# Gated cross-attention with a mixture of experts: score products in six single PSUM buffers, exponentials and maxima head by head, the two kinds of products interleaved

## The chip, the cores and the metric

The kernel runs on one core of a Trainium2 chip. A core has engines with instruction streams of their own: TensorE (PE in the profile; PEld are its weight loads), VectorE (DVE), ScalarE (ACT), GpSimd (POOL) and SyncE (SP, which here issues most DMAs). They wait for each other through semaphores. PE writes its products to PSUM, eight banks of 512 fp32 values in each of 128 partitions, and DVE and ACT read them from there. The metric is the device time of one execution in microseconds (us), as the median over runs.

## The reference, cut to what matters

```python
def reference(x, ctx_2048, g_xattn, g_ffn, ...):      # x, ctx: (8, 256, 512)
    x = x + tanh(g_xattn) * xattn(layernorm(x), ctx_2048, ctx_2048, ...)
    x = x + tanh(g_ffn) * moe(layernorm(x), ...)

def xattn(query, key, value, ...):                     # 16 heads of 16, sequence 512
    q, k, v = proj(Wq, query), proj(Wk, key), proj(Wv, value)
    q, k = rotary(q), rotary(k)
    scores = einsum('bdhn,bdhm->bhnm', q, k) / sqrt(16)
    prob = softmax(scores, axis=-1)
    x = einsum('bhnm,bdhm->bdhn', prob, v)
    return proj(Wm, x)

def moe(x, ...):                                       # 2048 tokens, 8 experts, top 2
    ...
    h = silu(x @ w0[e]) * (x @ w1[e]);  out += cw[e] * (h @ wo[e])
```

All is fp32. The softmax takes 8 x 16 heads with a 512 x 512 score matrix each.

## The kernel before

The kernel has two long stages: attention with routing (to about 605 us in the profile) and the experts (the rest). The change is in the first.

**Units and steps.** The 128 pairs of batch and head are cut into 32 units of four heads. The four heads of a unit lie on partitions 0, 32, 64 and 96 ("slots"), so that their products, whose contraction is over 32 partitions, sit in different rows of PE's array. A unit takes four steps, one for each block of 128 queries (or, in the second pass, of 128 keys). There are 128 steps. A batch is 16 steps.

**Two passes over the scores.** `scores(u, i, jp)` multiplies queries by keys for two heads (L803) and takes the maximum over the keys on DVE (L810, `tensor_reduce`, negated, into `nm`). `lower(u)` turns the maxima of a unit (L824) and sends them by four small DMAs (L827) into a spare row of the queries `qa`. `exponentials(u, mc, jp)` computes the scores again, transposed and with the maximum already subtracted by that row (L838), and ACT takes the exponential (L845) into `e`. `attend(u, mc)` multiplies `e` by the values and a column of ones (L855). The second pass runs `LAG` = 5 steps behind the first.

**Order by hand.** The loop at L1311 writes the order out, inside `manual_schedule`. Each step `t` has three places. Place 0 and place 1 end with one group of four score products: `exponentials` for two heads of the older unit, then `scores` for the two other heads of the newer unit, so that the four use all four slots:

```python
exponentials(t2 // NCH, t2 % NCH, place)
...
scores(t // NCH, t % NCH, 1 - place)
```

Ahead of each place stands other work, filed by `do(step, place, fn, ...)` and issued by `run`: its products first, then the rest. `attend` stands at place 1. At place 2 there is mostly one pair of projection, value or merge products (`turn` L610, `values` L780, `merge` L900) or transposes (`turn_half` L818) into the single bank `m`, evicted by ACT. On DVE the other work is: `attend`'s transposition of its result (L867), at place 1 once a unit; `normalise` (L878, L881) and `lower` (L824), at place 2 once a unit; `turn_back` (L891), at place 1 every second unit; `query_stats` and `token_stats` (L176, L177), one at place 1 and one at place 2, each once a batch; `own_both` (two instructions, L658) at place 2 twice a batch; and the router's small operations (L990 to L1087).

**PSUM.** The pool `ps_s` has three buffers of two banks each. A call of `scores` or `exponentials` takes one of them, fills both halves with two products, and has them read by one instruction of 1024 elements: the maximum or the exponential. Two further banks are `m` and `av`. Thus the buffer of a `scores` call is the one that the `exponentials` call of the group just before it had, and the buffer of an `exponentials` call is the one that the `scores` call two groups before had. `pair()` and `bank()` take from the same pool for the start, for the early expert rows and after the last step.

Of the kernel before, what the change touches and what calls it, by code (L numbers as in the profile page):

```python
# [8 lines left out]
FP = mybir.dt.float32  # L9
AF = mybir.ActivationFunctionType  # L10
ALU = mybir.AluOpType
AX = mybir.AxisListType
PSUM = bass.MemoryType.PSUM

P = 128
B, C, N = 8, 256, 512
H, HD = 16, 16
HG = P // HD
NG = H // HG
SLOT = 32  # L20
NS = P // SLOT
CC = C // P
NCH = N // P
UNITS = 2 * NG
E, M = 8, 1024
# [11 lines left out]
MOST, LEAST = max(CAPS), min(CAPS)  # L37
WHOLE = -(-MOST // SLOT) * SLOT
CT = MOST // P
# [12 lines left out]
def gated_cross_attention_moe(  # L52
# [19 lines left out]
    nc = tc.nc  # L72
# [19 lines left out]

    gw = const.tile([P, DC, SLOT], FP, tag="gw", name="gw")
    nc.gpsimd.memset(gw, 0.0)
    total = const.tile([P, E], FP, tag="total", name="total")
    nc.gpsimd.memset(total, 0.0)
    for i in range(NS):
# [5 lines left out]
            1.0,  # L103
            base=-i * SLOT,
            channel_multiplier=1,
# [37 lines left out]
    for par in range(2):  # L143
        nc.gpsimd.affine_select(
            spare[:, par, :],
            spare[:, par, :],
            [[-SLOT, NS]],
            ALU.not_equal,
# [82 lines left out]
    def tiles_of(n_rows):  # L231
        return [(j, min(P, n_rows - j * P)) for j in range(-(-n_rows // P))]
# [3 lines left out]
    class Rows:  # L236


        def __init__(self, pool, at, n_rows, most=0, once=None):
            self.n_rows, self.turned = n_rows, 0  # L240
            self.tiles = tiles_of(n_rows)
            self.n_blocks = -(-n_rows // SLOT)
            n_blocks = -(-max(most, n_rows) // SLOT)
# [191 lines left out]
    with ExitStack() as fill:  # L435
# [7 lines left out]
        r1 = prep.enter_context(tc.tile_pool(name="prep_1", bufs=1, side="right"))  # L443
        r2 = prep.enter_context(tc.tile_pool(name="prep_2", bufs=2, side="right"))
        r3 = prep.enter_context(tc.tile_pool(name="prep_3", bufs=3, side="right"))
        ps_s = fill.enter_context(tc.tile_pool(name="ps_s", bufs=3, space=PSUM, side="right"))
        ps_1 = ps_att.enter_context(tc.tile_pool(name="ps_1", bufs=1, space=PSUM))

        nobody = r1.tile([P, ROW], FP, tag="nobody", name="nobody")
# [9 lines left out]
        nm = wp.tile([P, NCH, 2, NS], FP, tag="nm", name="nm")  # L459
# [35 lines left out]
        others = p4.tile([P, NS, N], FP, tag="e", name="others")  # L495
# [31 lines left out]

        whole = slice(0, N)
        halves = slice(0, N // 2), slice(N // 2, N)
        banks = []  # L530
        spared = [False]
        where = ["m"]

        def bank():


            if not banks:
                if spared[0]:
                    banks.append(ps_s.tile([P, 2, N], FP, tag="s", name="s")[:, 0, :])
                else:  # L540
                    banks.append(ps_1.tile([P, N], FP, tag=where[0], name=where[0]))
            return banks[0]
# [20 lines left out]
        def constant_bias():  # L563

            ps = bank()
            for c in range(CC):
                for g in range(NG):
                    nc.tensor.matmul(
# [3 lines left out]
                        start=(g == 0),  # L572
                        stop=(g == NG - 1),
                    )
# [7 lines left out]
        xns, straight, turned, qs, ks, keys = {}, {}, {}, {}, {}, {}  # L582
        qas, es, avs_, outs, ats, pays = {}, {}, {}, {}, {}, {}
# [207 lines left out]
        def slot(j):  # L791
            return slice(j * SLOT, (j + 1) * SLOT)

        def spare_of(u):
            return HD * (1 - u % 2)

        def scores(u, i, jp):

            q, k = qs[u], ks[u]
            ps = ps_s.tile([P, 2, N], FP, tag="s", name="s")  # L800
            for j in range(2):
                sl = slot(2 * jp + j)
                nc.tensor.matmul(  # L803
                    ps[:, j, :],
                    lhsT=q[sl, i * P : (i + 1) * P],
                    rhs=k[sl, :],
                    start=True,
                    stop=True,
                )
            nc.vector.tensor_reduce(  # L810
                nm[:, i, u % 2, 2 * jp : 2 * jp + 2], ps, AX.X, ALU.max, negate=True
            )

        def turn_half(src, h, at=None):

# [13 lines left out]
                    in_=t[u % 2 * NS + j :: 2 * NS, :],  # L829
                )  # L830

        def exponentials(u, mc, jp):
            if (u, mc) not in es:
                es[u, mc] = p4.tile([P, NS, N], FP, tag="e", name="e")
            ps = ps_s.tile([P, 2, N], FP, tag="s", name="s")
            for j in range(2):
                sl = slot(2 * jp + j)
                nc.tensor.matmul(  # L838
                    ps[:, j, :],
                    lhsT=ks[u][sl, mc * P : (mc + 1) * P],  # L840
                    rhs=qas[u][sl, :],
                    start=True,
                    stop=True,
                )
            nc.scalar.activation(  # L845
                es[u, mc][:, 2 * jp : 2 * jp + 2, :], ps, AF.Exp, scale=float(HD**-0.5)
            )

        def attend(u, mc):
            b, g, par = u // UNITS, u // 2 % 2, u % 2  # L850
# [44 lines left out]
        def merge(b, c, cols):  # L895

            x_t = xres[b * CC + c]
            ps = bank()[:, : cols.stop - cols.start]
            for g in range(NG):
                nc.tensor.matmul(  # L900
# [3 lines left out]
                    start=(g == 0),  # L904
                    stop=(g == NG - 1),
                )
# [211 lines left out]
        LAG = NCH + 1  # L1118
        group_turns = ("k", 0), ("q", 0), ("k", 1), ("q", 1)
        for b in range(B):  # L1120
            t = b * per_batch


            if b:
                do(t - 16, 1, loads, b)
                i, i2 = (-14, -12) if b == 1 else (-15, -15)
# [14 lines left out]
            at = (-8, -7, -6, 1) if b == 1 else (-10, -9, -8, 1)  # L1141
            if b == 0:
                at = (3, 3, 4, 5)
            for mc, i in enumerate(at):
                do(t + i, 2 if b or mc == 1 else 1, values, b, mc, halves[0])
            for w in range(UNITS):
                u = UNITS * b + w
                s = t + w * NCH
# [9 lines left out]
            s = t + per_batch + LAG + 3  # L1158
            if b + 2 == B:
# [9 lines left out]
                at = "8.1 8.1 8.2 8.2 9.1 10.1 10.1 10.2 10.2 11.1"  # L1169
            else:  # L1170
# [8 lines left out]
                at = "15.1 15.2 16.1 16.2 17.1 17.2 18.1 18.2 19.1 19.2"  # L1179
# [29 lines left out]
        for i in range(3):  # L1209
            for c in range(NCH):  # L1210
                at = i * NCH + c
                do(2 * per_batch + at // 2 * NCH + at % 2, 0, part_of_weights, i, c)
        n_steps = B * per_batch
# [4 lines left out]
        t = AHEAD * per_batch + per_batch + LAG + 3  # L1218
# [75 lines left out]
            return t.unsqueeze(2 if t is limit else 1).to_broadcast(all_tiles)  # L1294

        def pair():
            ps = ps_s.tile([P, 2, N], FP, tag="s", name="s")
            return ps[:, 0, :], ps[:, 1, :]

        def early_work():  # L1300
            wg, wu, wout = firsts[0]
            r = early["rows"]
            yield from r.hidden(wg, wu, early["pool"], early["sg"], 1, pair, later)
            yield from r.project(wout, r.weights(0), lambda: pair()[0])
# [5 lines left out]
        with tc.manual_schedule():  # L1310
            for t in range(min(k[0] for k in beside), max(k[0] for k in beside) + 1):  # L1311
                for place in range(3):
                    spared[0] = t >= n_steps
                    where[0] = "av" if t < LAG and place == 2 else "m"
                    run(beside.pop((t, place), ()))
                    if place == 2:
                        continue
                    t2 = t - LAG
                    if 0 <= t2 < n_steps:
                        if t < n_steps:  # L1320
                            exponentials(t2 // NCH, t2 % NCH, place)
                        elif place == 0:
                            for jp in range(2):
                                exponentials(t2 // NCH, t2 % NCH, jp)
                    if LAG <= t < n_steps:
                        scores(t // NCH, t % NCH, 1 - place)
                    elif 0 <= t < LAG and place == 0:
                        for jp in range(2):
                            scores(t // NCH, t % NCH, jp)

            spared[0] = False
            b = B - 1
            work = early_work()
            normalise(UNITS * B - 1)
            turn_back(b, NG - 1)
            go(4)
            alone(merge, b, 0, whole)
            go(1)
            alone(merge, b, 1, whole)
            for c in range(CC):  # L1340
                token_stats(b, c)
            go(3)

            fn, args = held.pop(0)
            fn(*args)
            for c in range(CC):
                token_norm(b, c)
            go(6)
            full(token_turn, b, 0)
            go(1)  # L1350
            full(token_turn, b, 1)
            go(1)
            alone(consider, b)
            go(1)
            alone(choose, b)
            for fn, *args in router:
                if fn is count:
                    go(5)
                run([(fn, (b, *args))])
            holding[0] = False  # L1360
            flush()
            att.close()
            ps_att.close()

            w_odd = ctx.enter_context(tc.tile_pool(name="w_odd", bufs=1, reuse_waits="tile"))
            arrange()

            nc.vector.tensor_tensor(over, *map(by_tile, (limit, step)), ALU.add)
            nc.vector.tensor_tensor(
                lefts, taken.unsqueeze(2).to_broadcast(all_tiles), over, ALU.subtract  # L1370
            )
            nc.vector.tensor_scalar(there, lefts, 0.0, None, ALU.is_gt)
            nc.vector.tensor_reduce(n_over, there, AX.XY, ALU.add)
            nc.vector.tensor_copy(n_over_i, n_over)

            go(17)
# [359 lines left out]
```

## Time and profile before

| | |
|---|---|
| median of 3 runs | 1248.45 us (1246.9 to 1248.92) |
| the profiled execution's own time | 1244.89 us |
| its span, first to last instruction | 1243.2 us |
| granted PE clock | 0.996 of full |
| busy, share of the span | PE 98%, DVE 70%, PEld 60%, POOL 44%, ACT 35% |
| attention, 90 to 520 us: busy of 430 us | PE 429.8, DVE 325.7, ACT 254.5, POOL 183.6 |

PE is called busy from a product's start to its modelled end, so a product that waits while another runs beside it does not show as idle time. Shares over the whole span mix the two stages: DVE and ACT work most in the attention.

### The profile page before, as it was taken

To read this page: it belongs to the slowest core of one execution; us is meant where nothing else is said; L and a number is where in the kernel's file an instruction comes from. 1 tells how busy PE (TensorE), PEld (TensorE's weight loads), DVE (VectorE), ACT (ScalarE), POOL (GpSimd) and SP (SyncE) were. 2 spreads that over 40 slices of the span, in tenths; PEclk is the share of its full clock that TensorE was granted. 3 is DMA by queue.
4 is the path that set the end of the run, shared out by engine and by line. 5 is a ranking of instruction groups with operands and counts; after the bars stand their busy time and mean duration, and the time that the engine had idled before them with its cause. 6 is when DMAs were issued, how large, how long until landed. Compare 5 with 4: busy or idle time off the path is not lost. (4 is left out here: it accounts for less than half of the span.)

```text
span 1243.2 us, 18455 instructions
## 1 busy us (share of the span) xinstructions
PE 1221.7 (98%) x6768; PEld 747.8 (60%) x6768; DVE 869.2 (70%) x1638; ACT 431.2 (35%) x652; POOL 545.2 (44%) x654
## 2 busy tenths in 40 slices
PE   8999999999999999999999999999999999999996
PEld 5433343343433334333455778888888888888885
DVE  7676778777787777877432486686876868777673
ACT  3555655655565565655510110110101102021110
POOL 5413444515354360712122491754917548192631
PEclk9999999999999999999999999999999999999998
DMA  7440133312011110102155711621526126060100
GB/s 225 171 130 18 35 120 120 117 41 83 19 61 60 53 61 18 62 10 70 52 205 143 249 46 44 245 48 68 206 52 254 35 97 209 24 246 12 55 1 33
DMA packets 70651, 117.98 MB, mean 95 GB/s; under 512 B 14480, under 2 KB 33168, under 8 KB 70560
## 3 DMA queue, kind: packets, MB, share of 16 engines
q1 hardware_dynamic: 62528, 91.47, 22.7%
q0 software_dynamic: 8032, 25.32, 5.5%
q8 instruction: 54, 0.88, 0.3%
q14 instruction: 37, 0.30, 0.1%
HBM read 78.19 MB, written 31.00 MB: 88 GB/s over the span
## 5 line engine op out<-in xcount | busy, mean ns | idle before, releaser
L810 DVE TENSOR_REDUCE nm<-s 128x2 f32<-128x1024 f32 x256 | 311.1, 1220 | 131.1 <-PE s L803 130.9
L845 ACT ACTIVATE e<-s 128x1024 f32<-128x1024 f32 x256 | 261.5, 1023 | 183.7 <-PE s L838 101.1
L838 PE MATMUL s<-qa,k 32*128 32x512 f32 x1024 | 288.0, 639 | 1.4 <-DMA qa<-turned 1.3
L803 PE MATMUL s<-k,q 32*128 32x512 f32 x1024 | 283.6, 639 | 1.5 <-DVE q L658 1.0
L1516 PE MATMUL h<-hT,w 128*128 128x256 f32 (+4 forms) x672 | 168.0, 386 | 0.0
L1527 DVE TENSOR_TENSOR c<-u,h 128x256 f32<-128x256 f32 (+4 forms) x280 | 117.0, 423 | 71.8 <-PE h L1516 64.7
L838 PEld LDWEIGHTS s<-qa,k 32*128 32x128 f32 x1024 | 78.3, 183 | 146.7 <-issue 119.4
L415 POOL DMA_INDIRECT out_x<-y,tail x37 | 40.6, 1097 | 275.9 <-DVE y L1607 170.5
L1516 PEld LDWEIGHTS h<-hT,w 128*128 128x128 f32 x672 | 127.2, 190 | 23.3 <-DVE c L1527 1.8
L1532 ACT COPY u<-h 128x256 f32<-128x256 f32 (+4 forms) x70 | 26.3, 375 | 329.5 <-PE h L1516 279.3
L855 PE MATMUL av<-e,vones 128*32 128x512 f32 x1024 | 137.3, 605 | 0.2 <-ACT e L845 0.2
L1527 DVE TENSOR_TENSOR u<-u,h 128x256 f32<-128x256 f32 (+4 forms) x210 | 87.4, 424 | 60.3 <-PE h L1516 56.8
L1516 PE MATMUL h<-sum_h,sum_w 128*128 128x256 f32 (+4 forms) x448 | 108.6, 385 | 0.0
L916 POOL TENSOR_TENSOR x<-x,mrg 128x512 f32<-128x512 f32 x14 | 17.9, 1277 | 195.2 <-ACT mrg L912 194.2
L1516 PEld LDWEIGHTS h<-sum_h,sum_w 128*128 128x128 f32 x448 | 85.1, 190 | 14.3
L1576 ACT ACTIVATE c<-c 128x256 f32<-128x256 f32 (+4 forms) x112 | 46.1, 423 | 128.2 <-DVE c L1527 128.1
L1579 DVE TENSOR_TENSOR act<-c,c 128x256 f32<-128x256 f32 (+4 forms) x112 | 84.4, 754 | 3.8
L803 PEld LDWEIGHTS s<-k,q 32*128 32x128 f32 x1024 | 75.9, 183 | 9.0 <-ACT e L845 4.2
L855 PEld LDWEIGHTS av<-e,vones 128*32 128x32 f32 x1024 | 20.3, 108 | 98.2 <-issue 77.4
L1516 PE MATMUL h<-wo,act 128*128 128x256 f32 x336 | 77.5, 380 | 0.0
L1516 PEld LDWEIGHTS h<-wo,act 128*128 128x128 f32 x336 | 63.5, 190 | 9.5 <-issue 1.0
L1516 PE MATMUL h<-hT,sum_w 128*128 128x256 f32 (+4 forms) x224 | 59.1, 386 | 0.8 <-DVE c L1527 0.8
(227 smaller groups left out, 1697.7 us busy)
## 6 DMA issues: line engine op xcount, KB each, us to landing
w<-in_w SPq DMA_DIRECT2D x14, 2048.0 KB, 10.5
wo<-in_wo SPq DMA_DIRECT2D x7, 2048.0 KB, 15.9
rows<-nobody SPq DMA_DIRECT2D x8, 1042.0 KB, 5.7
swapped<-straight SPq DMA_DIRECT2D x60, 128.0 KB, 2.0
ctx<-in_kv SPq DMA_DIRECT2D x8, 512.0 KB, 5.7
x<-in_x SPq DMA_DIRECT2D x16, 256.0 KB, 3.0
out_x<-x SPq DMA_DIRECT2D x16, 256.0 KB, 2.0
w<-in_w SPq DMA_DIRECT2D x8, 512.0 KB, 3.9
```

Source lines behind the costliest of these rows:

```text
L415: scatter = nc.gpsimd.indirect_dma_start(out=out_rows, out_offset=bass.IndirectOffsetOnAxis(ap=self.ids[j], axis=0), in_=self.ys[j][: self ...
L803: nc.tensor.matmul(ps[:, j, :], lhsT=q[sl, i * P : (i + 1) * P], rhs=k[sl, :], start=True, stop=True,)
L810: nc.vector.tensor_reduce(nm[:, i, u % 2, 2 * jp : 2 * jp + 2], ps, AX.X, ALU.max, negate=True)
L838: nc.tensor.matmul(ps[:, j, :], lhsT=ks[u][sl, mc * P : (mc + 1) * P], rhs=qas[u][sl, :], start=True, stop=True,)
L845: nc.scalar.activation(es[u, mc][:, 2 * jp : 2 * jp + 2, :], ps, AF.Exp, scale=float(HD**-0.5))
L855: nc.tensor.matmul(avs_[u][slot(j), :], lhsT=vones[b % 2][:, mc, g * HG + 2 * j + par, :], rhs=e[:, j, :], start=(mc == 0), stop=(mc == NC ...
L916: (nc.vector if b == B - 1 else nc.gpsimd).tensor_tensor(x_t, x_t, t, ALU.add)
L1516: nc.tensor.matmul(ps, lhsT=left[:, c], rhs=right[:, c], start=(c == 0), stop=(c == k - 1))
L1527: nc.vector.tensor_tensor(z, x, y, ALU.add)
L1532: nc.scalar.copy(u1, p1)
L1576: nc.scalar.activation(c, c, AF.Silu)
L1579: nc.vector.tensor_tensor(r.act[:, NS * i + q, j * n : (j + 1) * n], sg[i, j], c, ALU.mult)
```

## The change

The pool has six buffers (`RING`) of one bank each. `take(n)` takes n of them. `both` replaces a call of `exponentials` and one of `scores` in every step in which both passes run: it takes four buffers and issues the products in turn, one of the second pass (`again`), one of the first (`score`), then again one of each. Each buffer is read by an instruction of its own, of 512 elements: `exponential` on ACT and `largest_of` on DVE, head by head. Where only one pass runs, `scores` and `exponentials` do the same with two buffers. `pair()` gives two of the six buffers, and `bank()`, where it used half of a double buffer, takes two and uses one. Nothing else is touched, and the other work keeps its steps and places.

```diff
+RING = 6
...
-        ps_s = fill.enter_context(tc.tile_pool(name="ps_s", bufs=3, space=PSUM, side="right"))
+        ps_s = fill.enter_context(tc.tile_pool(name="ps_s", bufs=RING, space=PSUM, side="right"))
...
+        def take(n):
+            return [ps_s.tile([P, N], FP, tag="s", name="s") for _ in range(n)]
...
+        def score(u, i, j, at):
+            nc.tensor.matmul(at, lhsT=qs[u][slot(j), i * P : (i + 1) * P],
+                             rhs=ks[u][slot(j), :], start=True, stop=True)
+        def largest_of(u, i, j, at):
+            nc.vector.tensor_reduce(
+                nm[:, i, u % 2, j : j + 1], at, AX.X, ALU.max, negate=True
+            )
...
-            nc.vector.tensor_reduce(
-                nm[:, i, u % 2, 2 * jp : 2 * jp + 2], ps, AX.X, ALU.max, negate=True
-            )
...
+        def exponential(u, mc, j, at):
+            nc.scalar.activation(
+                es[u, mc][:, j, :], at, AF.Exp, scale=float(HD**-0.5)
+            )
...
-            nc.scalar.activation(
-                es[u, mc][:, 2 * jp : 2 * jp + 2, :], ps, AF.Exp, scale=float(HD**-0.5)
-            )
...
+        def both(u, mc, u2, i, jp):
+            at = take(NS)
+            js = 2 * jp, 2 * jp + 1
+            others = 2 - 2 * jp, 3 - 2 * jp
+            for k in range(2):
+                again(u, mc, js[k], at[2 * k])
+                score(u2, i, others[k], at[2 * k + 1])
+            for k in range(2):
+                exponential(u, mc, js[k], at[2 * k])
+                largest_of(u2, i, others[k], at[2 * k + 1])
...
+                    if LAG <= t < n_steps:
+                        both(t2 // NCH, t2 % NCH, t // NCH, t % NCH, place)
+                        continue
```

More of the change, by code (lines that the diff above doesn't have):

```diff
@@ L538, in bank @@
                 if spared[0]:
-                    banks.append(ps_s.tile([P, 2, N], FP, tag="s", name="s")[:, 0, :])
+                    banks.append(take(2)[0])
                 else:
@@ L795, in spare_of @@
             return HD * (1 - u % 2)
+        def score(u, i, j, at):
+            nc.tensor.matmul(
+                at,
+                lhsT=qs[u][slot(j), i * P : (i + 1) * P],
+                rhs=ks[u][slot(j), :],
+                start=True,
+                stop=True,
+            )
[3 more added lines that the diff above has]
+            )
         def scores(u, i, jp):
-            q, k = qs[u], ks[u]
-            ps = ps_s.tile([P, 2, N], FP, tag="s", name="s")
+            at = take(2)
             for j in range(2):
[L802 to L808, printed above, removed]
-                )
-            nc.vector.tensor_reduce(
-                nm[:, i, u % 2, 2 * jp : 2 * jp + 2], ps, AX.X, ALU.max, negate=True
-            )
+                score(u, i, 2 * jp + j, at[j])
+            for j in range(2):
+                largest_of(u, i, 2 * jp + j, at[j])
         def turn_half(src, h, at=None):
@@ L830, in lower, with again, exponentials @@
                 )
-        def exponentials(u, mc, jp):
+        def again(u, mc, j, at):
             if (u, mc) not in es:
                 es[u, mc] = p4.tile([P, NS, N], FP, tag="e", name="e")
-            ps = ps_s.tile([P, 2, N], FP, tag="s", name="s")
-            for j in range(2):
[L837 to L845, printed above, removed]
-                es[u, mc][:, 2 * jp : 2 * jp + 2, :], ps, AF.Exp, scale=float(HD**-0.5)
-            )
+            nc.tensor.matmul(
+                at,
+                lhsT=ks[u][slot(j), mc * P : (mc + 1) * P],
+                rhs=qas[u][slot(j), :],
+                start=True,
+                stop=True,
+            )
+        def exponential(u, mc, j, at):
+            nc.scalar.activation(
+                es[u, mc][:, j, :], at, AF.Exp, scale=float(HD**-0.5)
+            )
+        def exponentials(u, mc, jp):
+            at = take(2)
+            for j in range(2):
+                again(u, mc, 2 * jp + j, at[j])
+            for j in range(2):
+                exponential(u, mc, 2 * jp + j, at[j])
+        def both(u, mc, u2, i, jp):
[8 more added lines that the diff above has]
+                largest_of(u2, i, others[k], at[2 * k + 1])
         def attend(u, mc):
@@ L1296, in pair @@
         def pair():
-            ps = ps_s.tile([P, 2, N], FP, tag="s", name="s")
-            return ps[:, 0, :], ps[:, 1, :]
+            return take(2)
         def early_work():
@@ L1318, in gated_cross_attention_moe @@
                     t2 = t - LAG
+                    if LAG <= t < n_steps:
+                        both(t2 // NCH, t2 % NCH, t // NCH, t % NCH, place)
+                        continue
                     if 0 <= t2 < n_steps:
-                        if t < n_steps:
-                            exponentials(t2 // NCH, t2 % NCH, place)
-                        elif place == 0:
+                        if place == 0:
                             for jp in range(2):
                                 exponentials(t2 // NCH, t2 % NCH, jp)
-                    if LAG <= t < n_steps:
-                        scores(t // NCH, t % NCH, 1 - place)
-                    elif 0 <= t < LAG and place == 0:
+                    if 0 <= t < LAG and place == 0:
                         for jp in range(2):
```

## The prediction

> **What bounds the kernel now.** I read the page first: PE is busy 98% of the span, and the score groups are among its dearest.
>
> ```profile
> PE 1221.7 (98%) x6768; PEld 747.8 (60%) x6768; DVE 869.2 (70%) x1638; ACT 431.2 (35%) x652; POOL 545.2 (44%) x654
> ...
> L810 DVE TENSOR_REDUCE nm<-s 128x2 f32<-128x1024 f32 x256 | 311.1, 1220 | 131.1 <-PE s L803 130.9
> L845 ACT ACTIVATE e<-s 128x1024 f32<-128x1024 f32 x256 | 261.5, 1023 | 183.7 <-PE s L838 101.1
> L838 PE MATMUL s<-qa,k 32*128 32x512 f32 x1024 | 288.0, 639 | 1.4 <-DMA qa<-turned 1.3
> ```
>
> DVE and ACT each idle before the scores, waiting for PE. PE's own waits hide in its busy time, so the timeline comes next (start, duration). One step:
>
> ```profile
> 300.37 0.70 PE L838 MATMUL s<-qa,k 32*128 32x512 f32 x2
> 300.38 0.70 PE L803 MATMUL s<-k,q 32*128 32x512 f32 x2
> ...
> 301.44 1.06 PE L855 MATMUL av<-e,vones 128*32 128x512 f32 x8
> 301.63 1.02 ACT L845 ACTIVATE e<-s 128x1024 f32<-128x1024 f32 x1 [0.68 <-PE s L803]
> 301.63 1.23 DVE L810 TENSOR_REDUCE nm<-s 128x2 f32<-128x1024 f32 x1 [0.98 <-PE s L803]
> ...
> 302.43 0.70 PE L838 MATMUL s<-qa,k 32*128 32x512 f32 x2
> ...
> 302.70 0.70 PE L803 MATMUL s<-k,q 32*128 32x512 f32 x2
> ```
>
> At place 0 (300.37) both kinds of products start within 0.01 us, and the next block starts 1.07 later. At place 1 (302.43) the scores start 0.27 late, because their buffer is free only when ACT's exponential ends, at 301.63 + 1.02 = 302.65. The row shows 0.05 from that end to PE's start, and the whole group is late by the 0.27.
>
> I took the time from each group's first product to the next block, less 1.07, over PE's whole timeline from 30 to 585 us. The 123 groups at place 1 lose 26.6 us, 96 of them 0.2 to 0.3 each. The 122 at place 0 lose 10.2 us, 105 of them nothing. Between 90 and 520 us, six regular batches, it is 22.0 and 0.6; the ends have 4.3 (30 to 90) and 9.8 (520 to 585). So 37 us is all that the change can take away. The rest of a step is products.
>
> **The change, part by part.**
>
> *First buffers free sooner.* A group now takes four of six buffers. Its first two products need what the group two back released; the last two need the first exponential and the first maximum of the group just before. Both sides of that are new: PE waited for DVE two groups back, now one back.
>
> *Exponential of 512.* Not in the trace. A copy of 256 from PSUM takes 0.37 and the exponential of 1024 takes 1.02, so 512 takes between those; on the line through both, 0.59. It ends 1.26 (301.63 − 300.37) + 0.59 + 0.05 = 1.90 after its group's start. The next group needs it 2.06 later (302.43 − 300.37): the place 1 wait goes, with 0.16 to spare. ACT gets 128 x 2 x (1.18 − 1.02) = 41 us more busy time, but 254 of 430 us is its load in the regular stretch, so that is covered. Were the cover gone, it would be 0.16 a group.
>
> *Maximum of 512.* Bounds: the 16-element reduction of the router takes 0.17, that of 1024 1.22; the line gives 0.69 at 512. Other DVE rows of 512 are 0.67 (L176), 0.71 (L867). I take 0.69. The first maximum is done at 1.26 + 0.69 + 0.05 = 2.00: 0.06 to spare at place 1, if DVE is free when the product ends.
>
> *What two cost DVE.* Instructions overlap at their ends: below, a maximum starting at 359.20 and lasting 1.19 is followed at 360.31, not 360.39. From all such pairs in the trace, 1024 occupy DVE 1.14, so 512 occupy 1.14 − 512/0.96 ns = 0.61, two of them 1.21. A step without waits has period 4.43 − 0.27 ≈ 4.15, of which four maxima take 2.43. That leaves DVE holes of 0.85 (its place 1 maxima to the next place 0 maxima) and 0.85 for the other work, which comes in bursts:
>
> ```profile
> 357.79 0.71 DVE L867 STREAM_TRANSPOSE avs<-av 128x512 f32<-128x512 f32 x1
> 358.42 0.65 DVE L176 BATCH_NORM_STATS2 st<-x 128x6 f32<-128x512 f32 x1
> 359.10 0.18 DVE L177 BATCH_NORM_AGGREGATE mv<-st 128x2 f32<-128x6 f32 x1
> 359.20 1.19 DVE L810 TENSOR_REDUCE nm<-s 128x2 f32<-128x1024 f32 x1
> ...
> 360.31 0.68 DVE L176 BATCH_NORM_STATS2 st<-x 128x6 f32<-128x512 f32 x1
> ...
> 364.59 2.55 DVE L658 TENSOR_SCALAR q<-a,own_col 128x512 f32<-128x512 f32 x2
> ...
> 367.06 2.34 DVE L810 TENSOR_REDUCE nm<-s 128x2 f32<-128x1024 f32 x2
> ```
>
> Before, such a burst delayed a buffer needed two groups later and cost nothing: these steps keep their period (the own queries at 364.59 make DVE do two maxima in a row at 367.06, and PE does not wait). Now the fourth product of the next group waits behind it, with everything behind that product on PE. Worked per batch, with a hole of 0.85:
> - own queries (L658), the pair that runs while POOL rotates: 2.55 less the hole is 1.7 late, less the 0.06 and what the preceding hole absorbs: 1.3. The batch's other pair takes 0.48 + 0.48, and fits.
> - transposition and first statistics at place 1: 0.63 + 0.78 occupy 1.41; 0.56 late, 0.4 on PE. Then the second statistics and `normalise` at place 2, 1.4 again: 0.57 on PE. Together 1.0.
> - the same with `token_stats`, one hole freer: 0.7.
> - `lower` comes 3.75 before the next unit's first second-pass product, where it had 3.7 to 4.3; its DMAs issue 0.28 and 0.86, in one unit of four 1.60 and 2.19, after it and land 1.7 later. So once a batch 0.15 late.
>
> Sum 3.1 a batch, six batches: +18.9. So the regular stretch gives −22.6 + 18.9 = −3.7. At the ends, where place 2 is empty or short, groups follow each other after 1.07 to 1.44, and PE waited 0.6 to 1.35 for a whole exponential; it now waits for the first maximum, 2.00 less that spacing, some 0.3 less for each of ten; the place 1 waits there (4.6) go but for one burst a side: −6. Sum −10 us. The profiled execution takes 1244.89 (span 1243.2 and 1.7 around it), 3.6 under the median; its change goes onto the median: 1248.45 − 10 = 1238.5. The expert stage is bound by PE and starts that much earlier.
>
> *More waits and releases on PE.* Each of the four products now has its own wait and release, where a pair had one. In the trace a wait that is met costs nothing seen: L803 starts 0.01 after L838 at 300.38 with a wait of its own. A score group releases two readers, `attend` at most one, and behind both the next block starts 0.07 before the modelled end (300.90 + 0.59 against 301.44; 301.44 + 1.06 against 302.43). I take zero. The nearest row for a dear one is PE's separate semaphore instruction, 51 ns.
>
> The Trainium skill, "TensorE: Matmul & The Clock Gate", section "The cost: per-tile semaphore tail", speaks against this part: each increment on a tile's completion adds 26.3 ns to the tail, so that one on the last is best. By it two more per group would be 2 x 26.3 ns x 246 = 13 us, and the sum +3 in place of −10, if the tail stood on PE's path; the trace's equal 0.07 behind one and two releases speaks against that.
>
> **The rivals.**
>
> *DVE becomes the bound, and it is slower.* If a 512 maximum occupies DVE for its whole 0.69 and not 0.61, four a step take 0.32 more. Some seven steps a batch are limited by DVE in my sum or on its edge: 7 x 0.32 x 8 = 18, so +8: 1256. It decides from 0.65, where the gain is gone. For it: DVE is at 325.7 of 430 already, and no maximum of 512 is in the trace. Against: every back-to-back row shows the overlap, the two maxima at 367.06 (2.34 for both) among them. Chance 0.16.
>
> *Waits and releases on PE.* At 51 ns for each of two more a group, 2 x 0.051 x 246 = 25 us: +15, 1263. It decides from 0.02 us each. Against it are the rows above. The skill's tail is this mechanism at a smaller price. Chance 0.05.
>
> *It does not matter.* The bursts take back all that the place 1 waits give, because place 1's 0.06 to spare is lost to a release some hundredths later and each burst carries over one group more: within 2.5 us of 1248. The wait has then only passed from ACT to DVE, and the change does not do what it says. Chance 0.13.
>
> *DVE absorbs the bursts.* If the slow pair of own queries is an accident of timing against POOL, and holes add up over two steps, most of the 18.9 does not come: −20 to −33, 1216 to 1228. For it: DVE's mean load after the change is still below the period. Chance 0.10.
>
> **How the numbers follow.** The forecast, −3 to −18, has 0.56; its own range is 1230 to 1245.5. With the absorbed case faster by over 0.2% (2.5 us, about what a measurement of this kernel tells from no change) has 0.66. Within it: 0.13. Slower: 0.21. The range takes the absorbed case's upper half below and DVE's price up to 0.67 above: 1224 to 1253.
>
> **What would show it.** Right: at place 1 all four products start within 0.02 in most steps, with 1.07 to the next block; the maxima are 512 wide at 0.65 to 0.69 and start 0.61 apart; PE's late fourth product, named as released by DVE, stands behind L658 and L176 alone; ACT shows no wait on it. Wrong: late fourth products in steps without bursts (maxima too dear), gaps over 1.08 behind groups that started together (releases), or bursts without a late product (absorbed).

## The result: 7 us less, and the profile after

The changed kernel takes 1240.61 us (median of five runs, 1238.73 to 1241.96). The kernel before, in five runs beside it, takes 1247.81 (1246.9 to 1248.92). The ratio is 0.9939 [0.9925, 0.9954], which is 7.2 us less. The profiled execution takes 1240.61, with a span of 1238.9.

The page of the changed kernel, first the busy time of the engines, then the lines that answer to those shown of before (`largest_of` is L812, `exponential` L855, `again` L846, `score` L803):

```profile
PE 1216.7 (98%) x6768; PEld 735.9 (59%) x6768; DVE 885.2 (71%) x1894; ACT 446.6 (36%) x908; POOL 545.4 (44%) x654
...
L812 DVE TENSOR_REDUCE nm<-s 128x1 f32<-128x512 f32 x512 | 328.1, 682 | 107.4 <-PE s L803 103.6
L855 ACT ACTIVATE e<-s 128x512 f32<-128x512 f32 x512 | 277.7, 594 | 171.3 <-PE s L803 134.1
L846 PE MATMUL s<-qa,k 32*128 32x512 f32 x1024 | 293.9, 639 | 1.9 <-DMA qa<-turned 1.9
```

Twice as many maxima and exponentials run, each a little over half as long. DVE is busier by 16.0 us and ACT by 15.4, and the kernel is faster all the same. The product of scores is as long as before, 639 ns. So the gain is in how the products stand, and that is read from the timeline. A step at place 1 without other work for DVE:

```profile
369.50 0.69 PE L846 MATMUL s<-qa,k 32*128 32x512 f32 x1
369.51 0.69 PE L803 MATMUL s<-k,q 32*128 32x512 f32 x1
369.52 0.69 PE L846 MATMUL s<-qa,k 32*128 32x512 f32 x1
369.52 0.69 PE L803 MATMUL s<-k,q 32*128 32x512 f32 x1
...
370.58 1.13 PE L614 MATMUL m<-xn,wq 128*128 128x256 f32 x4
```

All four products start within 0.02 us and the next block comes 1.08 later; before, L803 stood 0.27 behind L838 here. And a step at place 1 behind the own queries, whose two instructions are the 2.42 at the top:

```profile
362.25 2.42 DVE L662 TENSOR_SCALAR q<-a,own_col 128x512 f32<-128x512 f32 x2
363.04 1.35 POOL L645 TENSOR_TENSOR a<-a,swapped 128x512 f32<-128x512 f32 x1
...
364.17 0.69 PE L846 MATMUL s<-qa,k 32*128 32x512 f32 x1
364.18 0.69 PE L803 MATMUL s<-k,q 32*128 32x512 f32 x1
364.18 1.11 PE L846 MATMUL s<-qa,k 32*128 32x512 f32 x2
364.59 2.58 DVE L812 TENSOR_REDUCE nm<-s 128x1 f32<-128x512 f32 x4
...
365.33 1.12 PE L803 MATMUL s<-k,q 32*128 32x512 f32 x2
366.38 1.13 PE L614 MATMUL m<-xn,wq 128*128 128x256 f32 x4
```

Three products start at 364.17 to 364.18. The fourth comes at 365.33. It needs the buffer of the first maximum of the group before, and DVE cannot begin that maximum before 364.59, when the own queries end; it releases the buffer 0.68 later, at 365.27, and PE needs 0.05 more. The next block starts 2.21 after the group instead of 1.07. So one wait has gone from nearly every step, and another stands behind each burst on DVE.

The prediction's measure, each group's first product to the next block less 1.07, gives the balance. Here the 256 groups are compared by number, not by the clock, because the stretches end earlier in the changed kernel:

| groups (time in the kernel before) | lost before, us | lost after, us | difference | forecast |
|---|---|---|---|---|
| first 6 (to 30) | 1.11 | 2.18 | +1.07 | none |
| 27 (30 to 90) | 4.34 | 2.29 | −2.05 | −6, with 520 to 585 |
| 189 (90 to 520) | 22.60 | 19.68 | −2.92 | −3.7 |
| 29 (520 to 585) | 9.81 | 6.90 | −2.91 | in the −6 above |
| last 5 | 2.95 | 2.37 | −0.58 | none |
| sum | 40.81 | 33.42 | −7.39 | −9.7, given as −10 |

Two thirds of the gain stand at the ends (2.05 and 2.91), where DVE's bursts are few. From the first score product to the last group, the trace of before has 583.9 us and that of the changed kernel 576.7: −7.2, which is also the difference of the medians. The spans differ by only 4.3. In the changed kernel's profiled execution the first score product stands at 15.5 us and not at 14.2; the code up to there is the same, and in the ten profiled executions of this study it stands between 14.0 and 15.8. And its granted PE clock is 0.50 for 3.4 us from 632.4 us on, in the expert stage, which costs some 1.7 us; in the trace of before it is 1.00 throughout that stage.

### The profile page after: what moved, and what is told of

It is laid out like the page before. It is cut to its first block, busy times and chain, and to the rows that moved or that the text cites. A ratio compares the mean times of both kernels' runs of the same rounds, so it can differ in the third digit from the quotient of the medians.

```text
span 1238.9 us, 18902 instructions
## 1 busy us (share of the span) xinstructions
PE 1216.7 (98%) x6768; PEld 735.9 (59%) x6768; DVE 885.2 (71%) x1894; ACT 446.6 (36%) x908; POOL 545.4 (44%) x654
## 5 line engine op out<-in xcount | busy, mean ns | idle before, releaser
L812 DVE TENSOR_REDUCE nm<-s 128x1 f32<-128x512 f32 x512 | 328.1, 682 | 107.4 <-PE s L803 103.6
L855 ACT ACTIVATE e<-s 128x512 f32<-128x512 f32 x512 | 277.7, 594 | 171.3 <-PE s L803 134.1
L803 PE MATMUL s<-k,q 32*128 32x512 f32 x1024 | 312.6, 639 | 1.1 <-DVE q L662 1.0
L846 PE MATMUL s<-qa,k 32*128 32x512 f32 x1024 | 293.9, 639 | 1.9 <-DMA qa<-turned 1.9
L846 PEld LDWEIGHTS s<-qa,k 32*128 32x128 f32 x1024 | 82.1, 183 | 148.4 <-issue 115.7
L803 PEld LDWEIGHTS s<-k,q 32*128 32x128 f32 x1024 | 92.0, 183 | 12.9 <-DVE nm L812 9.3
```

Of the source, the lines that this page charges most:

```text
L803: nc.tensor.matmul(at, lhsT=qs[u][slot(j), i * P : (i + 1) * P], rhs=ks[u][slot(j), :], start=True, stop=True,)
L812: nc.vector.tensor_reduce(nm[:, i, u % 2, j : j + 1], at, AX.X, ALU.max, negate=True)
L846: nc.tensor.matmul(at, lhsT=ks[u][slot(j), mc * P : (mc + 1) * P], rhs=qas[u][slot(j), :], start=True, stop=True,)
L855: nc.scalar.activation(es[u, mc][:, j, :], at, AF.Exp, scale=float(HD**-0.5))
```

## The experiments

Theory A is the prediction's own: place 1 waited for a whole exponential of 1024; interleaving and single buffers take that wait away, and bursts on DVE then hold up the fourth product. All ratios are to the kernel before, which had a median of 1246.97 beside the first four runs and of 1246.94 beside the other four.

**The instructions alone.** Two kernels keep the double buffers and the order of before and only split the instructions, first the maximum:

```diff
-            nc.vector.tensor_reduce(nm[:, i, u % 2, 2 * jp : 2 * jp + 2], ps, ...)
+            for j in range(2):
+                at = 2 * jp + j
+                nc.vector.tensor_reduce(nm[:, i, u % 2, at : at + 1], ps[:, j, :], ...)
```

> The kernel before with one edit: each double buffer's maximum is taken by two instructions of 512 in place of one of 1024; buffers, product order and exponentials as before. Theory A (what counts is which instruction stands behind which buffer): the place 1 scores still wait for a whole exponential, 0.25 us a step, and a maximum is needed two groups later, so nothing changes: 1247.8, within 2. Rival B (DVE's own time counts: two maxima of 512 occupy it 0.61 each against 1.14 for one of 1024, 256 x 0.08 = 20 us more in all): slower by 5 to 20 us.

1250.02 us, ratio 1.0024 [1.0013, 1.0036], which is +3.0. The wait at place 1 is what it was (median 0.231 in both), and the regular stretch lost 23.2 instead of 22.6. So the split is nearly free there, but the total missed the expected 0 ± 2. In the profiled execution the rest sits at two places. At the start, the first group of the second pass loses 1.16 instead of 0.51, waiting for the rows that `lower` sends; the other kernels with split maxima lose 1.21 to 1.46 there (the changed one 1.39), and the one with split exponentials 0.50. And at about 575 us the last unit waits for the same rows, and then its products run at half speed:

```profile
575.12 1.24 PE L840 MATMUL s<-qa,k 32*128 32x512 f32 x4 [1.59 <-DMA qa<-turned]
576.38 1.99 PE L803 MATMUL s<-k,q 32*128 32x512 f32 x4
578.30 1.94 PE L857 MATMUL av<-e,vones 128*32 128x512 f32 x8
```

Windows of 1 us there, with the granted clock in the third column from the right:

```profile
575.00:576.00 1.00, 0.88 (x4) 0.44 (x4) 0.03 (x1) 1.00 (x2) 0.89 (x1) 1.00 0.02 2
577.00:578.00 1.00, 1.00 (x4) 0.00 (x0) 0.00 (x0) 0.94 (x2) 1.00 (x3) 0.50 0.44 171
```

The clock falls from 1.00 to 0.50 and is back before 584; over 575 to 584 it is 0.62, which costs about 9 x 0.38 = 3.4 us. Of this kernel's ten runs the median of the granted clock is 0.993, of the kernel before 0.995; 0.002 of 1247 is 2.5 us. So most of the +3 goes with a lower clock, and little is left for the price of the instructions. That the longer wait near the end let the clock fall is not shown: there is a trace of only one of the ten executions, and in other traces of this study the clock falls behind shorter waits and stays at 1.00 behind a longer one (last section).

Then the exponential, split in the same way (two `activation`s of 512, one for each half of the double buffer):

> The kernel before with one edit: each double buffer's exponential is taken by two ACT instructions of 512; buffers, product order and maxima as before. Theory A: the buffer is free only after the second, 1.26 + 0.49 + 0.60 + 0.05 = 2.40 us after the group's start, where the place 1 group needs it at 2.06: a wait of 0.34 in place of 0.25, about 100 times, so +9: 1257. Rival B (DVE's time counts): ACT has room, so no change: 1248 within 2.

1254.45 us, ratio 1.0054 [1.0038, 1.0071], +7.5. The wait at place 1 grew to a median of 0.292 from 0.231, and the regular stretch lost 27.9 instead of 22.6, because the buffer is free only when the second half is done: two take 0.49 + 0.59 = 1.08 from the first start to the last end, one took 1.02. Sign and place are A's; the expected 0.34 a group was 0.05 too much, and the +9 by 1.5.

**The buffers and the instructions, without the interleaving.** Six single buffers as in the change, but the two products of one kind follow each other again:

```diff
-                        both(t2 // NCH, t2 % NCH, t // NCH, t % NCH, place)
+                        exponentials(t2 // NCH, t2 % NCH, place)
+                        scores(t // NCH, t % NCH, 1 - place)
```

> The changed kernel with the interleaving undone alone: two products of the second pass, then two of the first, each pair with its two single buffers and two instructions. Then the last two products of a group stand behind the first and second exponential of the group just before, and no product behind a maximum nearer than two groups. Theory A: 0.34 us for the second exponential at place 1, about 100 times, and the late fourth products behind DVE's bursts go: slower than before by about 9, 1257. Rival B (DVE's time counts, wherever the buffers stand): the DVE bursts still cost their 20 us and the ACT wait adds to them only in other steps: 1265 or more. Rival C (single instructions and releases are what helps, the order does not matter): 1240.6 as in the changed kernel.

1249.17 us, ratio 1.0016 [1.0006, 1.0025]. That is 2.2 above before and, by the two ratios, some 10 above the changed kernel. So smaller buffers and instructions alone bring nothing: all of the gain needs the order in which the products take the buffers. C's 1240.6 and B's 1265 fall; A's 1257 has the right side, and is 8 too high, since the lag it took was 0.34 and 0.27 was measured. A step at place 1 of this kernel:

```profile
303.80 0.59 ACT L855 ACTIVATE e<-s 128x512 f32<-128x512 f32 x1
304.16 0.70 PE L846 MATMUL s<-qa,k 32*128 32x512 f32 x2
304.17 0.97 PE L803 MATMUL s<-k,q 32*128 32x512 f32 x2
```

The first L803 starts with L846, the second ends at 304.17 + 0.97 and so starts at 304.44: it waits for the second exponential, which ends at 303.80 + 0.59 = 304.39. The whole group is 0.27 late, as much as behind the one of 1024, and the place 1 groups of the regular stretch lose 23.6 us (median 0.268). In the interleaved order the fourth product takes a buffer that a maximum had, and no product takes the one of the second exponential of the group just before.

**The burst taken away.** If the slow pair of own queries costs 1.14 a batch, moving it to where POOL does not rotate takes that back:

```diff
-                    do(t + i, 1, rotate, b, "q", g)
+                    do(t + (4 if g else -6), 1, rotate, b, "q", g)
...
-                    do(t + i + 1, 2, own_both, b, g)
+                    do(t + (5 if g else -4), 2 if g else 1, own_both, b, g)
```

> The changed kernel with one edit to the order of other work: for the first group of heads of each batch the rotation of the queries on POOL and the two own-query instructions on DVE are issued two to three steps earlier, away from the rotation of the keys on POOL, and not all at place 2. Theory A: the pair takes 0.96 us in place of 2.6, and the fourth product that is 1.14 late once a batch behind it is on time: 7 x 1.1 = -8 against the changed kernel: 1232.5. Rival D (that stall is POOL's or PE's own and only stands beside the pair): 1240.6 within 2.

1232.76 us, ratio 0.9882 [0.9865, 0.9898]; 1232.5 was expected. The own queries from 90 to 520 us, as a group (busy time, mean ns), in the changed kernel:

```profile
L662 DVE TENSOR_SCALAR q<-a,own_col 128x512 f32<-128x512 f32 x24 | 19.8, 866 | 0.0
```

and in this one:

```profile
L662 DVE TENSOR_SCALAR q<-a,own_col 128x512 f32<-128x512 f32 x24 | 11.4, 516 | 0.0
```

The same 24 instructions take 866 ns on average where half of them stand beside POOL's rotation, and 516 away from it. The products that were late by 1.14 are gone, and the regular stretch loses 13.4 us instead of 19.7.

The next one also spreads the statistics: `query_stats` a step later, and `token_stats` and `token_norm` moved to places where `attend`'s transposition and `normalise` do not stand.

```diff
-                i, i2 = (-14, -12) if b == 1 else (-15, -15)
+                i, i2 = (-14, -12) if b == 1 else (-14, -14)
...
-                    do(s + 5, 1 + c, token_stats, b, c)
-                    do(s + 7, 1 + c, token_norm, b, c)
+                    do(s + 6 + c, 2 - c, token_stats, b, c)
+                    do(s + 7 + c, 2 - c, token_norm, b, c)
```

> The changed kernel with the earlier own queries of the run before, and the statistics of queries and tokens moved by one or two steps, to places where DVE has no transposition and no normalise. Theory A (the fourth product is late where DVE's other work is longer than its hole of 0.85 us): the two pairs of late fourth products a batch, 0.15 to 0.3 and 0.55 each, go: 7 x 1.4 = -10 against the run before, so 1223, about 17 below the changed kernel. Rival B (DVE's total time counts, not its bursts): as the run before, 1232.8, since DVE's work is only moved.

1230.09 us, ratio 0.9868 [0.9854, 0.9882]: the best version, 16.9 below the kernel before and by the two ratios 0.7% below the changed one. But 1223 was expected: of the 9.5 that the second step was to bring over the first, 2.7 came by the medians and 1.7 by the two ratios, whose intervals overlap. Rival B's 1232.8 is nearer than A's 1223, so by its time this run does not decide between them. The regular stretch loses 10.2 in place of 13.4, and the fourth product is still late by 0.34 to 0.49 where 0.55 stood. One reason shows at 352 us:

```profile
352.31 1.27 POOL L645 TENSOR_TENSOR a<-a,swapped 128x512 f32<-128x512 f32 x1
352.61 1.25 DVE L911 TENSOR_TENSOR o<-avs,rec 128x256 f32<-128x256 f32 x1
353.78 1.27 DVE L812 TENSOR_REDUCE nm<-s 128x1 f32<-128x512 f32 x2
354.12 0.69 PE L846 MATMUL s<-qa,k 32*128 32x512 f32 x1
354.51 0.69 PE L803 MATMUL s<-k,q 32*128 32x512 f32 x1
```

`normalise` (L911) takes 1.25 where it takes 0.42 in the changed kernel. POOL's rotation started 0.3 before it. The first maximum starts 0.8 later than it would, and the fourth product, at 354.51, is 0.39 behind the first. The other pair of own queries of each batch, whose place was not changed, shows the same at 387 us:

```profile
387.29 1.57 POOL L677 COPY qa<-a 128x512 f32<-128x512 f32 x2
387.56 1.58 DVE L662 TENSOR_SCALAR q<-a,own_col 128x512 f32<-128x512 f32 x2
389.79 0.69 PE L803 MATMUL s<-k,q 32*128 32x512 f32 x1
```

Beside the two copies on POOL they take 0.83 each where they took 0.48, and the fourth product, at 389.79, is 0.46 behind the group's first. Over the regular stretch `normalise` takes 698 ns on average in this kernel and 425 in the changed one; the own queries, at 516 in the run before, are back at 675. So a burst that is moved must miss POOL's work as well as DVE's.

**The same moves in the kernel before.** They could help by themselves, whatever the buffers:

> The kernel before with the same moves of own queries and statistics. Theory A: there the maxima are needed two groups later, bursts cost nothing, and the moves bring nothing: 1247, within 2. Rival E (the moves help by themselves, on POOL or in the chain of routing, not through the fourth product): about 15 faster here as well.

1246.75 us, ratio 1.0004 [0.9994, 1.0014]. They bring nothing there, so the bursts matter only once a buffer is due one group later. The rival E falls.

**A burst added.** Three reductions of 512 elements, whose result is not used, once a batch (`wm_s` lies in SBUF), first in the changed kernel:

```diff
+        def probe():
+            for _ in range(3):
+                t = p1.tile([P, 1], FP, tag="probe", name="probe")
+                nc.vector.tensor_reduce(t, wm_s.rearrange("p c o -> p (c o)"), AX.X, ALU.max)
...
+                do(t - 4, 2, probe)
```

> The changed kernel with added work: once a batch, at place 2 of a step where DVE has none of its other work, three reductions of 512 elements whose result is not used, 1.83 us. Theory A: the hole is 0.85, so the fourth product of the next place 1 is 1.83 - 0.85 - 0.06 = 0.92 late, seven or eight times: +6.5, 1247. Rival B (DVE's total time counts): 8 x 1.83 = 15 us of DVE time in a stage where it is at 79%: below +2 if there is room, up to +15 if not.

1245.93 us, ratio 0.9997 [0.9989, 1.0006]. Against the changed kernel's 0.9939 that is +7.2 us, where A gave +6.5. The whole gain is gone with three short instructions a batch, on an engine that is busy for 340 of the 430 us of the regular stretch in the changed kernel. That stretch loses 25.8 instead of 19.7. The added loss stands where A has it: in each of the seven batches the fourth product behind the reductions makes its group 0.83 to 0.96 late, where A gave 0.92. Rival B allowed 7 us too, but names no such place.

And in the kernel before:

> The kernel before with the same three added reductions once a batch. Theory A: a maximum is needed only two groups later, so 1.83 us of more DVE work in a free step cost nothing: 1247, within 2. Rival B: the same cost as in the changed kernel.

1249.6 us, ratio 1.0023 [1.0014, 1.0032], +2.8 where A gave 0 ± 2 and B the +7.2 of the run above. So the older order absorbs more than half of a burst, not all:

```profile
357.94 0.69 DVE L1123 TENSOR_REDUCE probe<-wm 128x1 f32<-128x512 f32 x1
...
366.47 2.55 DVE L658 TENSOR_SCALAR q<-a,own_col 128x512 f32<-128x512 f32 x2
368.95 2.34 DVE L810 TENSOR_REDUCE nm<-s 128x2 f32<-128x1024 f32 x2
370.21 0.70 PE L838 MATMUL s<-qa,k 32*128 32x512 f32 x2 [0.52 <-DVE nm L810]
```

From the probe on DVE has no hole up to 370 us; each later burst (statistics, `normalise`, own queries) adds to the delay until, 12 us on, the buffer needed two groups later is late too. It delays a whole group, here by 0.52 at 370.21, and so once a batch: the time between one group's work and the next group's first product grows by 3.5 us over the trace, while within the groups the regular stretch loses 21.8, no more than before. Slack of one group more is a larger store, and a dense row of bursts empties it.

## Why the prediction was right

It gave 1238.5 and 1240.6 was measured, a change of −7.2 where −10 was forecast. Step by step:

- *Durations.* Exponential of 512: 0.59 forecast, 0.594 measured. Maximum of 512: 0.69 forecast, 0.682. Occupancy of two maxima: 1.21 forecast from the overlap; in most pairs they start 0.607 apart (1.29 for two). The rival that DVE becomes the bound needed 0.65 and falls. One time was too long in the sum: the exponential and the maximum were to start 1.26 after their group's first product, as with double buffers. In steps without a late product they start after 1.16 and 1.20, since the first no longer waits for the second product, so the maximum had 0.13 to spare at place 1 and not 0.06.
- *The place 1 wait goes.* Shown: the median of place 1 is 0.000 where it was 0.231, and the timeline above is one of 145 groups of some 190 in the regular stretch, both places together, that lose less than 0.05 (97 before). The waits of the regular stretch have changed hands to DVE's bursts, but a gain of 2.9 is left, so "it does not matter" falls. "DVE absorbs the bursts" falls too.
- *What the bursts give back.* 3.15 a batch forecast, 3.1 measured in the batch that begins at 357 us, but not in the same shares. Own queries 1.14 (1.3 forecast); transposition, statistics and `normalise` 0.23 + 0.55 = 0.77 (1.0); the same with `token_stats` 0.14 + 0.55 = 0.69 (0.7); `lower` nothing that shows (0.15); and the router 0.25 + 0.30, which the sum did not have (a product, L1066, that waits for a DVE operation behind `attend`'s transposition, then a fourth product behind the router's small operations and `normalise`). The right total was partly luck. Over the stretch it is 19.7 against 18.9. The two experiments that move bursts away confirm the mechanism, the last two show it from the other side.
- *Waits and releases.* Forecast at nothing. With four waits and four releases a group, the next block still comes 1.07 to 1.08 after the first product (369.50 to 370.58), as with two of each. The Trainium skill, "TensorE: Matmul & The Clock Gate", section "The cost: per-tile semaphore tail", gave the prediction an estimate of 13 us for this; the trace shows no part of that on PE's path. The rival falls.
- *The ends.* Mis-sized: −6 forecast for 30 to 90 and 520 to 585, −5.0 measured. Most groups that follow each other closely lose 0.2 to 0.5 less, where 0.3 was forecast (0.581 became 0.270 in one of them), but two in the last unit lose as much as before or more (1.125 became 1.370, 0.942 became 0.949).
- *The start.* +1.1, with no term in the sum. DVE limits the first groups there, four maxima take 2.48 where two took 2.36, and PE then waits longer between two heads' rows: their products start 1.40 apart (30.76 and 32.16) where it was 0.51. That the split of the maxima brings it is shown by the experiment that does only that; why the rows then land further apart is not.

So the difference from the forecast is 0.8 in the regular stretch, 1.0 at the ends and 1.1 at the start, less 0.6 in the last five groups.

## What to carry to other kernels

Which instruction a buffer's next user waits for depends on the order of taking as much as on the number of buffers: the same six buffers and the same small instructions gained nothing until the products were interleaved. Freeing buffers sooner takes slack away elsewhere, so list the bursts on the engine that releases them and weigh each against the hole in its step before making the change; moving those bursts afterwards gave more here (9 us by the two ratios) than the change itself (7 us). Compare traces group by group and not by the clock, since an early gain shifts every later window.

## What the runs showed of the hardware

- **POOL stretches DVE.** DVE operations from SBUF to SBUF take two to three times as long when a tensor operation on POOL runs beside them: the own queries 2.42 for two in place of 0.48 each, `normalise` 1.25 in place of 0.42; beside POOL's copies the own queries take 0.83 each. The Trainium skill, "SBUF — State Buffer", section "SBUF: two separate sides", gives a lock for this: VectorE and GpSimd share a port pair that one holds for a whole instruction. The trace agrees in the size: `normalise` started 0.97 before POOL's instruction ended, and took 0.83 more. Maxima, which read PSUM, keep their 0.68 beside POOL.
- **Instructions overlap at their ends.** A maximum of 512 lasts 0.68 and the next starts 0.61 after it; an exponential lasts 0.59 and the next starts 0.49 after it. Sums of durations overstate an engine's load by a tenth to a fifth at this size.
- **PE's clock can fall to half behind a short wait, and the wait's length does not decide it.** After the wait of 1.59 us shown above the granted clock was 0.50 for 6.8 us. In the trace of the changed kernel it was 0.50 for 3.4 us soon after a wait of 2.16 at 629 us, and in that of the grouped order for 3.4 us from 577.9 on, after a wait of 0.86 that ended at 575.0; in the kernel before a wait of 2.38 at 635 us left it at 1.00. The Trainium skill, "TensorE: Matmul & The Clock Gate", section "What's actually happening", has PE fall to half after an idle window of about 3.4 us; no wait here was as long as that, while the times at half clock are one such window or two. What decides is not shown. A stretch at half clock can cost more than the wait ahead of it: 6.8 us at 0.50 are about 3.4 us of PE's work lost.
